# Four-layer graph network, layer 1: maximum over eight blocks, factors in two parts, negation on GpSimd, norms and skips at other items

## The chip, the cores and the metric

The kernel runs on one core of a Trainium2 chip. The metric is device time in microseconds of one execution; the time before is the median of three runs. The engines are named as in the profile: PE is TensorE's matmul and PEld its weight load, DVE is VectorE, ACT is ScalarE, POOL is GpSimd and SP is SyncE, which issues the DMAs.

## The reference

Four layers, each added to its input and followed by a layer norm over the 128 features. There are 3125 nodes and 103125 directed edges. Layer 0 is a weighted sum over neighbours. Layer 1, which the change touches, is an attention over edges with four heads of 32 features:

```python
h = (x @ W).reshape(n, HEADS, C)
a_s = jnp.einsum('nhc,hc->nh', h, att_src)
a_d = jnp.einsum('nhc,hc->nh', h, att_dst)
e = jax.nn.leaky_relu(a_s[src] + a_d[dst], NEG_SLOPE)
p = jnp.exp(e - m[dst])                      # m: the segment's maximum
out = segment_sum(h[src] * (p / z[dst])[:, :, None], dst)   # z: segment sum of p
out = out + gat_bias + x @ skip_W + skip_b
out = (out - mu) * rsqrt(var + EPS_LN) * ln_g + ln_b
x = layernorm(x + out)
```

Layer 2 is a dot-product attention and layer 3 two mean aggregations with a sigmoid.

## The kernel before, in words

The edges are turned into dense matrices: `wd` holds the weighted adjacency for layer 0 and `f_ctd` the edge counts (bf16) for layers 1 to 3. Nodes lie in 25 blocks of 128, `NB`. `general_path` is a fallback that doesn't run here; all the work is `fast_path`.

**Layer 0 to layer 1.** Layer 0's sums of blocks 0 to 19 (`Z0` = 20) end first; those of blocks 20 to 24 (`acc1`, tiles `left0` and `left1`) are still to be added from source blocks `ZA` = 6 to 24. The loop `for i in range(NB)` adds them (`add0`, line L862) and runs layer 1's preparation between, by a table `marks` of what is to be done at which `i`. `end0` adds the residual (L874) and normalises x. `scores1(g)` takes four blocks: transposes x (L1047), multiplies by the attention vectors (L1292, L1299), copies the destination scores out (L1301) and stores them to DRAM (L1302). `heads` copies the source scores to `sa` (L1307). `top` takes their maximum over all 20 blocks (L1401, then `highest` and `spread` by way of TensorE, L1081 to L1091), which gives `km`, the number that is subtracted ahead of the exponentials. The result doesn't depend on it as long as no exponential overflows; `in_range` looks after that. `factors` makes the exponentials of 20 blocks at once (L1315 to L1329).

`values(b)` makes the product operand `vp` of two blocks: x times W (L1336), scaled by the two factors (L1340), then split into three bf16 parts, each a cast on ScalarE and a subtraction on VectorE (L565 to L570 in `split3`), and last, a negated copy of the second half of the columns (L1350, one instruction a block). Eight pairs are made in the loop over `i`, at 9, 11, ..., 23, and five more inside head 0.

**The items.** Layer 1 then runs over `items` (g, h, c): two groups of destination blocks (`IG`, 12 and 13), four heads, 25 source blocks c: 200 items. `masks` makes for an item which edges take which branch of the leaky ReLU: an ACTIVATE on ScalarE (L1384) and a minimum on VectorE (L1388), or for some items one instruction on VectorE (L1380); one item in five of the later heads also has L1391. `products` multiplies count matrix and mask with `vp` (L1449, L1453), summing in PSUM over c. At the end of a head, `sums` reduces (L1482) and GpSimd finishes (L1490 to L1495); `quotients` divides nine items later (L1499 to L1505, items of 1.6 to 1.9 us).

`later(k, f)` puts `f` into a list that `step()` runs k items later; what step() starts stands behind the last mask and product already issued on its engine. `skips` (L1463, L1466) computes x times `skip_W` for four blocks at a time into `r`. `finished` runs the norms of group 0 under the items of group 1: `finish1` for four blocks is a first norm (L1116 to L1120, a root on ScalarE, then L1209 and L1210) and a second norm with its scaling on ScalarE (L1141) or, with `on_v`, on VectorE (L1134). `turns1` transposes the new x (L1150) and multiplies by layer 2's weights (L1158). `unit`, `doubled` (L1258) and `bound2` prepare layer 2. PSUM's banks are named acc0 to acc4, tr_sa, left0 and left1; `bank()`, which highest, skips and turns use, is acc1 alone in layer 1.

What order the instructions take on an engine is set by the framework's scheduler from readiness and from the order of the program; `tc.issue_after(i)` puts the instructions of a block behind `i` on that engine.

Of the kernel before, what the change touches and what calls it, by code (L numbers as in the profile page):

```python
# [13 lines left out]
OP = mybir.AluOpType  # L14
AX = mybir.AxisListType
# [4 lines left out]
NB = 25  # L20
# [499 lines left out]
def fast_path(  # L520
# [351 lines left out]
    def end0(acc, b0, n):  # L872
        i = x[:, b0 : b0 + n, :]
        nc.vector.scalar_tensor_tensor(i, acc[:, 0:n, :], 0.0, i, OP.max, OP.add)  # L874
        layer_norm(lp0, i, i, (0, n), True)

    zp = front.enter_context(tc.tile_pool(name="f_zp", bufs=4))
# [186 lines left out]
    def later(k, f):  # L1064
        due.append((now[0] + k, f))
# [21 lines left out]
    def spread(d, n, o):  # L1087

        t = bank()
        nc.tensor.matmul(t[:, 0:n], ones, d, start=True, stop=True)  # L1090
        nc.vector.tensor_copy(o, t[:, 0:n])  # L1091
# [168 lines left out]
    with ExitStack() as st:  # L1260
# [43 lines left out]
        def heads(t, b0, n):  # L1304

            b = slice(b0, b0 + n)
            nc.vector.tensor_copy(sa[:, b, :], t[:, 0 : n * 2 * H].rearrange("p (b h) -> p b h", h=2 * H))  # L1307
            nc.vector.tensor_scalar(nas[:, b], sa[:, b, 0:H], -1.0, None, OP.mult)
            nc.gpsimd.tensor_scalar(bas[:, b], sa[:, b, 0:H], UP, None, OP.mult)
# [21 lines left out]
        def values(b):  # L1331
# [17 lines left out]
            for k in range(n):  # L1349
                nc.vector.tensor_scalar(  # L1350
                    vp[:, b + k, :, :, 2 * F1 : 3 * F1], vp[:, b + k, :, :, F1 : 2 * F1], -1.0, None, OP.mult
                )
# [41 lines left out]
        spare.append(lambda: zps.tile([P, 512], F32, name="few", tag="acc1"))  # L1394
        marks = {ZA - 1: lambda: [scores1(g) for g in range(Z0 // 4)]}
        keep = {}

        def top():
            heads(t8, 0, Z0)
            ex = fp.tile([P, H], F32, name="ex", bufs=1)  # L1400
            nc.vector.tensor_reduce(ex, sa[:, 0:Z0, 0:H].rearrange("p b h -> p h b"), AX.X, OP.max)  # L1401
            keep["d"] = highest(fp, ex, H)

        marks[ZA] = top
        marks[ZA + 2] = lambda: (spread(keep["d"], H, km), factors(0, Z0))
        ready = 0
        for i in range(NB):
            if i >= ZA:
                add0(cp, i, acc1, (Z0, NB - Z0), "ct1")
            if i in marks:  # L1410
                marks[i]()
            if i in (19, 21, 23):
                masks(*items[(i - 19) // 2])
            if i > ZA + 2 and i % 2:
                values(ready)
                ready += 2
        sp = st.enter_context(tc.tile_pool(name="f_sp1", bufs=2))
# [4 lines left out]
        for g, (b0, n) in enumerate(left):  # L1422
            end0(acc1[g], b0, n)
        def in_range():
# [48 lines left out]
        def sums(acc, g, h):  # L1473
# [39 lines left out]
            def finished():  # L1513
                for k, b in enumerate(range(0, n, 4)):
                    later(15 * k, lambda b=b: finish1(sp, i0 + b, min(4, n - b), 2, False))
                    later(15 * k + 12, lambda b=b: turns1(sp, i0 + b, min(4, n - b), 5))
                later(2, lambda: unit(i0, n))
                later(58, lambda: doubled(i0, n))
                later(57, lambda: bound2(sp, 0))

            later(1 if last else 9 if g or h else 18, quotients)
            if (g, h) == (0, H - 1):
                later(20, finished)

# [3 lines left out]
        for x_, (g, h, c) in enumerate(items):  # L1528
# [4 lines left out]
            if (g, h, c) == (0, 1, 0):  # L1533
                lag[0] = 4
            if (g, h, c) in ((0, 1, 0), (1, 0, 1)):
                later(0, lambda: skips(i0, i0 + n))
            if (g, h, c) == (0, 2, 12):
# [19 lines left out]

            if c < NB - 1:
                more_masks()
# [492 lines left out]
```

## Time and profile before

| | |
|---|---|
| median of 3 runs | 1314.13 us (1310.74 to 1314.8) |
| profiled execution | 1310.76 us, of which the span of instructions is 1309.0 us |
| busy, share of the span | PE 94%, PEld 84%, DVE 73%, ACT 66%, POOL 22% |
| mean granted TensorE clock | 0.993 |
| layer 0's last sums, blocks 0 to 19 | end at 409.5 us |
| layer 1's products | 446.9 to 805.8 us |
| ends of heads (first and last L1482), group 0 | 499 to 505, 542 to 546, 580 to 584, 618 to 621 us |
| ends of heads, group 1 | 663 to 668, 712 to 718, 761 to 765, 801 to 806 us |
| set of norms of group 0 (first L1116 of each `finish1`) | 657.9, 688.4, 719.0 us |

The profile is of one execution. "Busy" of TensorE includes matmuls that are pipelined, so its idle time is the sure reading; the idle time stands in the timeline in brackets ahead of an instruction, with the name of what ended it. A stretch's row gives its length, then the busy time and count of each engine, the granted clock, the DMA engines' share and GB/s.

### The profile page before, as it was taken

The page shows a single profiled execution, that of the slowest core. Times are in us where ns is not written, and L with a number is a line of the kernel's source. Part 1 is how long each engine was busy: PE and PEld are TensorE (multiplying, and loading weights), DVE is VectorE, ACT ScalarE, POOL GpSimd, SP SyncE. Part 2 cuts the span into 40 slices and gives each one's busy share as a digit, 9 for nine tenths or more (in the row PEclk, how much of TensorE's full clock was granted, in tenths as well). Part 3 has the DMA queues.
Part 4 walks back from the last instruction along what each step waited for, and adds up shares of the span by engine and source line. Part 5 has one row for each costly group of instructions (what it writes and reads, how often), then busy time and mean ns, then how long its engine had stood idle before and what let it go on. Part 6 is the DMA issues. An engine that isn't in the chain of part 4 may idle for free.

```text
span 1309.0 us, 31168 instructions
## 1 busy us (share of the span) xinstructions
PE 1235.2 (94%) x13072; PEld 1102.6 (84%) x13072; DVE 953.5 (73%) x1420; ACT 866.1 (66%) x1364; POOL 284.5 (22%) x219
## 2 busy tenths in 40 slices
PE   4999999999999998999989999999999999999995
PEld 3899999999997888999989897777777777876785
DVE  6989999999934898899889987843474347332365
ACT  2977787777744797999788996544474444543455
POOL 6904526091002242222211322000000000000011
PEclk9999999999999999999999999999999999999998
DMA  7579898988997766888877775522222223861674
GB/s 184 148 223 285 239 273 264 277 258 252 289 307 235 252 206 212 282 282 281 252 250 237 236 244 175 199 68 73 62 75 76 75 64 101 258 205 49 203 220 134
DMA packets 192261, 261.95 MB, mean 200 GB/s; under 512 B 16844, under 2 KB 135802, under 8 KB 191982
## 3 DMA queue, kind: packets, MB, share of 16 engines
q1 hardware_dynamic: 191085, 257.42, 64.1%
q8 instruction: 104, 1.70, 0.5%
q0 software_dynamic: 720, 1.97, 0.5%
q10 hardware_dynamic: 305, 0.48, 0.1%
q14 instruction: 47, 0.39, 0.1%
HBM read 196.72 MB, written 63.10 MB: 198 GB/s over the span
## 4 chain that ended last, share of the span: by engine, by line
PE 70%; DVE 11%; ACT 8%; DMA 3%; issue 3%; POOL 1%; SPq 1%; POOLq 0%; DVEq 0%; ACTq 0%
PE acc L1453 11%; PE acc L1672 11%; PE s L1664 10%; PE wp L961 7%; PE acc L1449 6%; PE acc L862 6%; PE acc L1772 5%; PE cp L953 3%; PE acc L1854 3%; ACT wod L925 2%; DVE cm L1388 2%; ACT cm L1384 2%; ACT cs L966 1%; DVE wod L918 1%; DMA ct<-f_ctd 1%
## 5 line engine op out<-in xcount | busy, mean ns | idle before, releaser
L1449 PE MATMUL acc<-vp,ct 128*128 128x99 bf16 (+1 forms) x2500 | 323.2, 209 | 7.6 <-DVE vp L1350 5.1
L1453 PE MATMUL acc<-vp,cm 128*128 128x198 bf16 (+1 forms) x2500 | 324.6, 244 | 5.2 <-DVE cm L1388 5.1
L1384 ACT ACTIVATE cm<-adr,bas 128x1536 bf16<-128x1536 f32 (+1 forms) x184 | 286.4, 1619 | 31.4 <-PE acc L1453 22.3
L1453 PEld LDWEIGHTS <-cm 128*128 128x128 bf16 x2500 | 239.6, 97 | 16.4 <-issue 8.8
L1449 PEld LDWEIGHTS <-ct 128*128 128x128 bf16 x2500 | 242.2, 98 | 1.1 <-DVE ct L1391 0.6
L1388 DVE TENSOR_TENSOR cm<-cm,ct 128x1536 bf16<-128x1536 bf16 (+1 forms) x184 | 195.3, 1087 | 24.3 <-ACT cm L1384 20.0
L1668 DVE TENSOR_TENSOR e<-e,ct 128x512 f32<-128x512 f32 (+2 forms) x175 | 107.5, 623 | 105.3 <-ACT e L1667 100.5
L1667 ACT ACTIVATE e<-s,f_nm 128x512 f32<-128x512 f32 (+2 forms) x175 | 109.4, 633 | 109.4 <-PE s L1664 105.1
L961 PE MATMUL wp<-wod,ohc 128*128 128x128 f16 x2512 | 167.7, 220 | 14.8 <-ACT cs L966 12.2
L1672 PEld LDWEIGHTS acc<-self__6449,e 128*128 128x128 f32 x1250 | 147.4, 192 | 21.5 <-issue 13.1
L961 PEld LDWEIGHTS <-ohc 128*128 128x128 f16 x2512 | 149.1, 98 | 15.7 <-issue 15.2
L918 DVE TENSOR_TENSOR wod<-ohd,w 128x4096 f16<-128x4096 f16 (+1 forms) x82 | 161.6, 2009 | 0.0
L1672 PE MATMUL acc<-self__6449,e 128*128 128x129 f32 x1250 | 147.9, 275 | 1.8 <-DVE e L1668 1.8
L862 PE MATMUL acc<-f_xw,cw 128*128 128x128 f32 x1000 | 143.6, 284 | 4.1 <-DMA cw<-wd 4.1
L1664 PE MATMUL s<-yT,f_xT 128*128 128x512 f32 (+2 forms) x350 | 140.0, 539 | 0.1
L862 PEld LDWEIGHTS acc<-f_xw,cw 128*128 128x128 f32 x1000 | 123.6, 193 | 4.7 <-DMA cw<-wd 4.7
L966 ACT CAST cs<-cp 128x500 bf16<-128x500 f32 x157 | 90.4, 576 | 51.5 <-PE cp L953 50.6
L1615 ACT CAST cr<-ct 128x1590 fp32r<-128x1590 bf16 (+3 forms) x51 | 72.3, 1418 | 76.8 <-PE acc L1772 39.0
L925 ACT ACTIVATE wod<-ohd,wt 128x128 f16<-128x128 f16 x312 | 106.5, 398 | 9.5 <-DVE ohd L907 9.4
L1664 PEld LDWEIGHTS s<-yT,f_xT 128*128 128x128 f32 x350 | 62.8, 190 | 48.4 <-issue 21.5
L972 ACT COPY ws<-wp 128x512 f32<-128x512 f32 x157 | 88.0, 585 | 17.1 <-PE wp L961 17.0
L1617 DVE CAST cr<-ct 128x1536 fp32r<-128x1536 bf16 (+2 forms) x59 | 53.8, 915 | 62.5 <-PE acc L1772 31.5
(355 smaller groups left out, 1697.8 us busy)
## 6 DMA issues: line engine op xcount, KB each, us to landing
ct<-f_ctd SPq DMA_DIRECT2D x186, 384.0 KB
ct<-f_ctd SPq DMA_DIRECT2D x100, 416.0 KB
wd<-ws SPq DMA_DIRECT2D x39, 896.0 KB
cw<-wd SPq DMA_DIRECT2D x50, 640.0 KB
f_ctd<-cs SPq DMA_DIRECT2D x9, 2000.0 KB
ct<-f_ctd SPq DMA_DIRECT2D x25, 397.2 KB
ct<-f_ctd SPq DMA_DIRECT2D x22, 397.5 KB
ct<-f_ctd SPq DMA_DIRECT2D x25, 269.5 KB
```

What stands on the lines that cost most here:

```text
L862: steps.append(lambda j=j, a=cw[:, j - h, :]: nc.tensor.matmul(accs[j // 4][:, j % 4, :], a, xw[:, i, :], start=False, stop=(i == NB - 1 a ...
L918: tip[s] = nc.vector.tensor_tensor(packed(f, ww), packed(ohd, ww), twos(w2[s])[:, ww], OP.mult)
L925: nc.scalar.activation(wod[1][:, BW + w, :], ohd[:, BW + w, :], AF.Copy, scale=wl[:, 1, at : at + 1])
L961: tip["made"] = made = nc.tensor.matmul(wp[:, j, :], ohc[:, w, :], wod[s][:, w, :], start=(j == 0 and q == 0 and s == 0), stop=(j == 3 and ...
L1384: pins["a"] = nc.scalar.activation(m[:, : n * P], adrs[g, h][:, : n * P], AF.Relu, bias=bas[:, c, h : h + 1], scale=UP)
L1388: pins["v"] = nc.vector.tensor_tensor(m[:, : n * P], m[:, : n * P], ct[:, : n * P], OP.min)
L1449: nc.tensor.matmul(out_(F1, w), ct[:, k * P : (k + 1) * P], vp[:, c, h, :, 2 * F1 : F1 + w], start=(c == 0 and k % 2 == 0), stop=False, sk ...
L1453: pins["p"] = nc.tensor.matmul(out_(0, z), m[:, k * P : (k + 1) * P], vp[:, c, h, :, 0:z], start=False, stop=(c == NB - 1 and (k % 2 == 1 ...
L1664: nc.tensor.matmul(s[:, :m], xT[:, c * P : (c + 1) * P], yT[:, i0 * P + a : i0 * P + a + m], start=True, stop=True)
L1667: nc.scalar.activation(e[:, a : a + m], s[:, :m], AF.Exp, bias=nm[:, q : q + 1], scale=scale)
L1668: nc.vector.tensor_tensor(e[:, a : a + m], e[:, a : a + m], ct[:, a : a + m], OP.mult)
L1672: nc.tensor.matmul(acc[k // 3][:, (k % 3) * (P + 1) : (k % 3 + 1) * (P + 1)], es[q, c][:, k * P : (k + 1) * P], vo[:, c, 0 : P + 1], start ...
```

## The change

- `top` takes `heads` and the maximum over the first eight blocks, after two calls of `scores1`; the other three come at i = 8, 10 and 12, `heads` of blocks 8 to 19 at 13. `factors` runs for blocks 0 to 7 at i = 7 and for 8 to 19 at i = 14.
- Pairs of values are made at i = 8, 9, 11, 13, 15, 16, 18, 20 and 22: nine instead of eight.
- The negation L1350 goes from VectorE to GpSimd.
- `end0` gives back its addition, and the masks issued in the first three items stand behind the last of these on its engine.
- `finished` starts 10 items after the sums instead of 20. `finish1` starts at 0, 18 and 43 from there (before 0, 15, 30), with its second scaling on VectorE; `turns1` at 19, 43 and 50 (before 12, 27, 42); `bound2` and `doubled` at 68 and 70 (before 57 and 58).
- The skips of group 1's blocks run at the start of head 3 of group 0 instead of in item 1 of group 1.

```diff
     def end0(acc, b0, n):
         i = x[:, b0 : b0 + n, :]
-        nc.vector.scalar_tensor_tensor(i, acc[:, 0:n, :], 0.0, i, OP.max, OP.add)
+        added = nc.vector.scalar_tensor_tensor(i, acc[:, 0:n, :], 0.0, i, OP.max, OP.add)
         layer_norm(lp0, i, i, (0, n), True)
+        return added
...
             b = slice(b0, b0 + n)
-            nc.vector.tensor_copy(sa[:, b, :], t[:, 0 : n * 2 * H].rearrange("p (b h) -> p b h", h=2 * H))
+            z = b0 * 2 * H if b0 < Z0 else 0
+            nc.vector.tensor_copy(sa[:, b, :], t[:, z : z + n * 2 * H].rearrange("p (b h) -> p b h", h=2 * H))
...
             for k in range(n):
-                nc.vector.tensor_scalar(
+                nc.gpsimd.tensor_scalar(
                     vp[:, b + k, :, :, 2 * F1 : 3 * F1], vp[:, b + k, :, :, F1 : 2 * F1], -1.0, None, OP.mult
                 )
...
-        marks = {ZA - 1: lambda: [scores1(g) for g in range(Z0 // 4)]}
         keep = {}
 
         def top():
-            heads(t8, 0, Z0)
+            heads(t8, 0, 8)
             ex = fp.tile([P, H], F32, name="ex", bufs=1)
-            nc.vector.tensor_reduce(ex, sa[:, 0:Z0, 0:H].rearrange("p b h -> p h b"), AX.X, OP.max)
+            nc.vector.tensor_reduce(ex, sa[:, 0:8, 0:H].rearrange("p b h -> p h b"), AX.X, OP.max)
             keep["d"] = highest(fp, ex, H)
 
-        marks[ZA] = top
-        marks[ZA + 2] = lambda: (spread(keep["d"], H, km), factors(0, Z0))
+        def more_values():
+            nonlocal ready
+            values(ready)
+            ready += 2
+
         ready = 0
+        marks = {ZA - 1: lambda: [scores1(g) for g in range(2)], ZA: top}
+        marks[ZA + 1] = lambda: (spread(keep["d"], H, km), factors(0, 8))
+        marks[ZA + 2] = lambda: (more_values(), scores1(2))
+        marks[ZA + 3] = more_values
+        marks[ZA + 4] = lambda: scores1(3)
+        marks[ZA + 5] = more_values
+        marks[ZA + 6] = lambda: scores1(4)
+        marks[ZA + 7] = lambda: (more_values(), heads(t8, 8, Z0 - 8))
+        marks[ZA + 8] = lambda: factors(8, Z0 - 8)
+        for i in (15, 16, 18, 20, 22):
+            marks[i] = more_values
...
-            if i > ZA + 2 and i % 2:
-                values(ready)
-                ready += 2
...
         for g, (b0, n) in enumerate(left):
-            end0(acc1[g], b0, n)
+            added = end0(acc1[g], b0, n)
...
             def finished():
-                for k, b in enumerate(range(0, n, 4)):
-                    later(15 * k, lambda b=b: finish1(sp, i0 + b, min(4, n - b), 2, False))
-                    later(15 * k + 12, lambda b=b: turns1(sp, i0 + b, min(4, n - b), 5))
+                for b, k, t in zip(range(0, n, 4), (0, 18, 43), (19, 43, 50)):
+                    later(k, lambda b=b: finish1(sp, i0 + b, min(4, n - b), 2 if k < 43 else 1, True))
+                    later(t, lambda b=b: turns1(sp, i0 + b, min(4, n - b), 5))
                 later(2, lambda: unit(i0, n))
-                later(58, lambda: doubled(i0, n))
-                later(57, lambda: bound2(sp, 0))
+                later(70, lambda: doubled(i0, n))
+                later(68, lambda: bound2(sp, 0))
...
-                later(20, finished)
+                later(10, finished)
...
-            if (g, h, c) in ((0, 1, 0), (1, 0, 1)):
-                later(0, lambda: skips(i0, i0 + n))
+            if (g, h, c) in ((0, 1, 0), (0, 3, 0)):
+                later(0, lambda of=IG[h // 2]: skips(of[0], sum(of)))
...
-            if c < NB - 1:
+            if x_ < 3:
+                with tc.issue_after(added.ins):
+                    more_masks()
+            elif c < NB - 1:
                 more_masks()
```

## The prediction

> **What bounds the kernel now.** I read the page first, then busy time by stretch, cut at the reductions L1482 that end each head, then TensorE's timeline for the idle places, then groups by line for the prices.
>
> The page's first part says which engine to follow:
>
> ```profile
> PE 1235.2 (94%) x13072; PEld 1102.6 (84%) x13072; DVE 953.5 (73%) x1420; ACT 866.1 (66%) x1364; POOL 284.5 (22%) x219
> ```
>
> TensorE is busy 94% of the span, so the change can win only where TensorE waits. Layer 1's products run from 447 to 806 us. By stretch (length, then PE, PEld, DVE, ACT and POOL busy; PEclk is the granted clock):
>
> ```profile
> 447.00:503.00 56.00, 48.14 (x616) 45.05 (x614) 50.60 (x104) 46.70 (x58) 15.12 (x22) 0.94 0.64 200
> ...
> 584.00:621.00 37.00, 37.00 (x599) 37.00 (x596) 34.21 (x37) 35.26 (x25) 12.43 (x6) 1.00 0.88 288
> 621.00:668.00 47.00, 47.00 (x692) 46.95 (x690) 40.47 (x49) 35.22 (x23) 9.76 (x7) 1.00 0.81 254
> 668.00:718.00 50.00, 44.71 (x678) 43.35 (x676) 46.14 (x92) 43.26 (x44) 9.00 (x9) 1.00 0.74 235
> 718.00:765.00 47.00, 44.15 (x661) 43.04 (x659) 43.35 (x74) 41.11 (x44) 12.41 (x8) 1.00 0.72 226
> ```
>
> The first row is head 0 of group 0: TensorE idles 56.00 - 48.14 = 7.9 us and the clock is below 1, while VectorE is busy 50.6 of 56. The last four are head 3 of group 0 and heads 0, 1, 2 of group 1. TensorE loses nothing until 668, then 5.3 and 2.9 us, where VectorE is busy 46 of 50 and 43 of 47. These two places, 16 us of idle time, are what the change touches. TensorE's timeline says what it waited for:
>
> ```profile
> 451.49 0.25 PE L1449 MATMUL acc<-vp,ct 128*128 128x102 bf16 x1 [2.20 <-DVE f_x L874]
> 456.47 0.26 PE L1453 MATMUL acc<-vp,cm 128*128 128x198 bf16 x1 [0.48 <-DVE cm L1388]
> 487.70 0.21 PE L1449 MATMUL acc<-vp,ct 128*128 128x102 bf16 x1 [1.46 <-DVE vp L1350]
> 492.20 0.21 PE L1449 MATMUL acc<-vp,ct 128*128 128x102 bf16 x1 [1.16 <-DVE vp L1350]
> 498.09 0.21 PE L1449 MATMUL acc<-vp,ct 128*128 128x102 bf16 x1 [2.53 <-DVE vp L1350]
> 675.10 0.26 PE L1453 MATMUL acc<-vp,cm 128*128 128x198 bf16 x1 [3.09 <-DVE cm L1388]
> 730.28 0.26 PE L1453 MATMUL acc<-vp,cm 128*128 128x198 bf16 x1 [1.57 <-DVE cm L1388]
> ```
>
> In head 0 the last releaser is always VectorE: layer 0's last addition L874, which stood in its queue behind values; a mask; and three times the negation L1350 that ends a pair of values. The two in group 1 are masks late behind norms (L1209, L1210 stand just before at 669 and 727 us). Two idle places also cost clock:
>
> ```profile
> 451.40:454.70 3.30, 3.21 (x26) 3.01 (x26) 3.30 (x15) 1.86 (x4) 0.00 (x0) 0.50 0.18 73
> ...
> 499.10:502.50 3.40, 3.40 (x30) 3.16 (x29) 1.73 (x4) 0.07 (x1) 0.00 (x0) 0.50 0.31 116
> ```
>
> For 3.3 and 3.4 us after the waits of 2.20 and 2.53 the granted clock was 0.50, so some 1.7 us each is lost again. After the longer wait of 3.09 us at 672 the clock stayed at 1.00. The Trainium skill (TensorE: Matmul & The Clock Gate, Part 1) says that the clock is judged in free-running windows of about 3.4 us; by that rule it is chance which gap is punished. Recoverable in all: 7.9 + 3.4 + 8.1 = 19.4 us.
>
> **The change, part by part.**
>
> *Maximum over eight blocks, factors in two parts.* Before, the copy L1307 of the scores comes at 422.99, after all five groups, and the first value product L1340 at 427.26, 4.3 us later. Group 1's scores leave TensorE at 415.2 (L1299, 414.17 + 1.02), so now the first value can come at 415.2 + 4.3 = 419.5. What can delay it: the transpose in `highest` uses bank acc1, which group 1's L1299 fills and ScalarE's L1301 empties, before only at 418.88 to 419.44; from there (L1081 to L1340, 3.3 us) it is 422.8. So values start 4.5 to 7.7 us earlier; I take 6. VectorE has room: it idled 1.81 us before 415.64 and 5.70 us before 422.99. TensorE gains nothing before 447: L862 fills it there, and its work is only reordered. The added work is one more heads (about 0.3 + 0.2 us) and one more set of factors, under 2 us on VectorE and 1.1 us on ScalarE, in time that was idle. A wait of TensorE for acc1 could cost up to 3 us; L862 steps stand ready beside it, and I charge 0.8.
>
> In head 0, VectorE is relieved of what spilled past 447 (one L1340, two L567, three L569, at 0.41, 0.75 and 0.75 us: 4.2 us) and of one whole pair, since nine pairs instead of eight now stand ahead of the products (two L1340, one L567, one L569: 2.3 us). 50.6 - 6.5 = 44.1 us. TensorE's own work there is 56 - 7.9 - 3.4 - 0.4 (the pair's four L1336) = 44.3 us. The two come out level, so the waits shrink but don't all go. I take the 2.20 us behind L874 as gone with its clock loss of 1.65, and the 0.48. Of the last three waits (5.15 us) I keep 3: the last four pairs are issued at the same steps as before, four items (4 x 1.6 us) ahead of use, and their chain (L1340 0.8, then L565, L567, L568, L569, L570 at 0.63 to 0.75, then the negation) takes about as long. Half of the second clock loss goes, 0.85. Sum: 2.20 + 1.65 + 0.48 + 2.15 + 0.85 - 0.8 = **6.5 us**, between a loss of 3 (the acc1 wait, nothing else) and a gain of 11.3.
>
> *Negated values on GpSimd.* VectorE sheds 25 L1350, 5.8 us busy. GpSimd's price isn't in the trace. From below: its L1309 on 128x80 takes 0.42 us; from above, L733 and L736, one-input steps on 128x256, average 2.3 and 2.5 us while VectorE is saturated. The nearest rows are L1344 (128x256, 0.70) and L1490 (128x396, 1.55, two inputs); I take 0.9, so 22.5 us in all. It isn't free for VectorE: at 505.20 five L1388 took 6.49 us, 1.30 each, with GpSimd working beside them, against 0.95 alone. That is 0.27 us per us of GpSimd, or 6.1 us for 22.5: it eats the 5.8 saved. At 0.42 us each VectorE would gain 3; at 2.4 each it would lose 10. I put it at **0**. What it moves: a pair now ends with two GpSimd steps, 1.8 us instead of 0.45, part of the 3 us that I kept above.
>
> The Trainium skill (GPSIMD Engine Reference, 4.1 Engine selection, and 1. Specifications) speaks against this edit: element-wise work belongs on VectorE, and GpSimd shares its SBUF interfaces. It calls one-input work roughly line-rate. As an estimate from its 3.1, 396 elements at 1.8 cycles and 1.2 GHz take 0.6 us, by which the edit would win VectorE about 1.7 us.
>
> *`added`, masks of the first three items behind it.* Masks L1388 from 455.5 already stand behind L874 (454.63): 0, and nobody waits longer.
>
> *Norms between the changes of heads.* A set of four blocks costs VectorE, by groups from 621 to 765: L1116 1.7, L1118 0.7, L1120 0.8, L1209 1.9, L1210 1.4, reciprocals 0.3: 6.9 us. With the second scaling on VectorE instead of ScalarE (four times 0.34, as L1134 takes at 837 us) it is 8.2; ScalarE sheds 4 x 0.41 = 1.65 us a set (L1141 at 682). Sets now start 10, 28 and 53 items after the group's change instead of 20, 35 and 50, so one falls in each of heads 0, 1 and 2; in the kernel before head 1 holds nearly two. VectorE afterwards: head 0: 40.5 - 2.3 (skips) - 1.9 (L1116 and others already there) + 8.2 = 44.5 against TensorE's 47.0 - 1.5 = 45.5. Head 1: 46.1 - 6.0 (four of twelve L1116 and L1118, four of eight L1209 and L1210) + 1.4 = 41.5 against 44.7. Head 2: 43.4 + 1.4 = 44.8 against 44.2. So TensorE leads in two and VectorE by half a us in the third. Of 8.1 us idle I keep 3: **5 us** gained, between 0 and 8. The first set stands one item behind the quotients' GpSimd steps (L1501, L1505, some 3 us), so VectorE may wait a us for them; that is in the 3.
>
> *All skips in group one.* Thirteen L1463 (1.5 us of TensorE) and four L1466 (2.3 us of VectorE) move from 631 us to head 3 of group 0. TensorE's work is only moved. VectorE there goes from 34.2 to 36.5 of 38.5 us: cover enough. The wait for a skip's bank can recur (1.0 us at 513): I charge 0.5, between 0 and 1.2.
>
> **Sum.** 6.5 + 0 + 5 - 0.5 = 11 us. The profiled execution took 1310.76 us (span 1309.0), so 1299.8 on its own scale. That is 3.4 below the median of the three runs, 1314.13, and at their low end. On the median's scale 1314.1 - 11 = **1303** us is my number.
>
> **Rivals.**
> *GpSimd sets the pace (slower).* GpSimd works in order. If a pair's negations stand ahead of the next pair's copies L1343, the pairs no longer overlap: 0.8 + 1.9 of casts + 1.5 of subtractions + 0.4 to 0.8 of copies + two negations + waits between engines, about 6.4 us a pair at 0.9 each. Thirteen pairs from 420 end at 503, 5 us behind today's 498.3, just what the norms gain. That is the point from which it decides: above 0.9 us each, in order, it is a loss. At 1.2 us: 7.0 x 13 = 91, last value at 511, 13 late; 13 - 5 = 8 slower, 1322. Against it: today copies of the next pair (427.86) already run ahead of L1344 of the last (428.82), so the order interleaves.
> *Nothing gained (same).* The stalls only move: head 0 stays tied to the last four pairs' chain, VectorE is as late with masks in head 2, and 3 us or less are won: 1312.
> *One half works.* Only head 0 or only the norms: 5 to 6 us, 1308 or 1309. For it: the two stages share nothing but VectorE.
>
> **How the numbers follow.** Both halves 0.50; one half 0.20; nothing 0.14; slower 0.16. Faster by over 0.3% (4 us, about what a measurement of this kernel can tell from no change) is the first two, 0.70; within it 0.14; slower 0.16. The low end, 1295, takes nearly the whole 19.4 us. The high end, 1316, takes in the case of nothing gained and the mild end of the slow one.
>
> **What would show it.** Right: no half clock near 451; products from about 447 as now, head 0's L1482 near 496 instead of 499 to 505; first L1340 near 421; idle time of TensorE from 668 to 765 halved, group 1's last L1482 some 11 us earlier. Wrong: L1449 released by GpSimd in long waits, negations over 1.2 us each, L1388 means above 1.1 us in head 0, new waits of TensorE for bank acc1 at 415 to 420, or a mask late behind L1134-like scalings in head 2.

## The result and the profile after

The changed kernel takes 1319.72 us in the median of 18 runs (1314.22 to 1321.74); the kernel before took 1314.42 us beside it (18 runs, 1310.74 to 1318.94). The ratio is 1.0038, with a 95% interval of 1.0029 to 1.0047: about 5 us slower, where 11 us faster was forecast, and outside the range given (1295 to 1316).

The profiled execution took 1319.73 us, of which the span is 1317.8, at a mean granted clock of 0.988. That is 9.0 us over the profiled execution of before, which was one of that kernel's quickest. Part of the gap doesn't belong to the change: layer 0's sums end at 412.0 instead of 409.5 us, with one half-clock window (403.3 to 406.7) just before. So the two traces are compared below from layer 0's end on, stage by stage. The page's first part, after:

```profile
PE 1237.7 (94%) x13072; PEld 1104.1 (84%) x13072; DVE 959.2 (73%) x1413; ACT 862.3 (65%) x1356; POOL 320.3 (24%) x246
```

TensorE is as busy as before; GpSimd has 36 us more, 25 of its 27 new instructions being the negations. Line numbers moved a little: the negation is L1352 (L1350 before), the copies of factors L1345 (L1343), the self product L1346 (L1344), masks L1386, L1390 and L1393 (L1384, L1388, L1391), products L1462 and L1466 (L1449, L1453), sums L1495 (L1482), skips L1476 and L1479 (L1463, L1466), turns L1151 and L1159 (L1150, L1158), the copy of a turn's result L1168 (L1167), the scaling on VectorE L1135 (L1134), masks in one instruction L1382 (L1380).

Busy time by stretch, after: length, then PE, PEld, DVE, ACT and POOL busy, granted clock, DMA share, GB/s. The rows are head 0 of group 0 with what runs into it, head 3 of group 0, and heads 0, 1 and 2 of group 1:

```profile
449.40:510.70 61.30, 49.61 (x654) 46.57 (x653) 50.96 (x89) 51.30 (x62) 37.30 (x42) 0.94 0.61 190
592.60:632.10 39.50, 38.08 (x593) 37.88 (x591) 34.51 (x40) 33.63 (x23) 6.01 (x5) 1.00 0.79 251
632.10:675.20 43.10, 43.10 (x651) 43.10 (x649) 41.48 (x68) 33.76 (x24) 9.77 (x7) 1.00 0.84 274
675.20:722.00 46.80, 43.69 (x670) 42.61 (x668) 44.18 (x75) 39.75 (x35) 12.55 (x9) 1.00 0.76 249
722.00:774.40 52.40, 48.76 (x678) 46.49 (x676) 44.89 (x77) 41.28 (x44) 14.47 (x9) 0.93 0.65 205
```

Head 0 still leaves TensorE idle for 61.30 - 49.61 = 11.7 us, more than the 7.9 before, and GpSimd, which was busy 15 of 56 us there, is busy 37 of 61. Group 1's head 2 has 52.40 us, with 3.6 idle and the clock at 0.93. In TensorE's timeline after, the instructions that stood longest, with the idle time and its releaser in brackets:

```profile
457.43 0.25 PE L1462 MATMUL acc<-vp,ct 128*128 128x102 bf16 x1 [5.15 <-DVE f_x L874]
462.40 0.21 PE L1462 MATMUL acc<-vp,ct 128*128 128x102 bf16 x1 [1.76 <-DVE f_x L874]
500.38 0.21 PE L1462 MATMUL acc<-vp,ct 128*128 128x102 bf16 x1 [3.33 <-POOL vp L1352]
599.30 1.13 PE L1476 MATMUL few<-f_l_swt,f_xT 128*128 128x128 f32 x8 [1.42 <-DVE f_xw L1479]
742.35 0.22 PE L1462 MATMUL acc<-vp,ct 128*128 128x99 bf16 x1 [1.33 <-DVE ct L1393]
745.73 1.08 PE L1151 MATMUL few<-f_ident,f_x 128*128 128x128 f32 x4 [1.88 <-DVE self__6449 L1168]
```

The wait behind L874, which the forecast took as gone, is there and larger (2.20 before, 5.15 and 1.76 now). The waits for the last pairs, whose releaser is now GpSimd's negation, add up to 4.5 us (5.15 before, of which the forecast kept 3), the longest 3.33 (2.53). Two are new and have to do with bank acc1: a skip in head 3 of group 0 and a turn in head 2 of group 1. Around the first wait the clock is at half (same columns as the stretches above):

```profile
403.30:406.70 3.40, 3.40 (x19) 3.40 (x18) 2.02 (x10) 0.00 (x0) 0.00 (x0) 0.50 1.13 221
454.50:461.30 6.80, 3.22 (x24) 2.82 (x24) 4.35 (x10) 3.45 (x7) 6.33 (x10) 0.50 0.21 86
```

The first row is the window in layer 0 named above; the second lies across the end of the 5.15 us wait.

In us from layer 0's end, the lengths of the stages by the ends of the last reduction of each head, for before, after, and three kernels of the experiments below:

| | before | after | a_neg_dve | c_turns | d_skips6 |
|---|---|---|---|---|---|
| to the end of head 0, group 0 | 95.8 | 98.6 | 91.3 | 91.3 | 91.3 |
| heads 1 and 2 | 79.1 | 79.4 | 79.5 | 78.9 | 79.4 |
| head 3 (skips of group 1 are now here) | 37.4 | 42.0 | 42.0 | 41.9 | 40.4 |
| group 1, head 0 | 46.5 | 43.1 | 43.1 | 43.1 | 43.1 |
| head 1 | 49.9 | 46.6 | 46.6 | 47.8 | 47.9 |
| head 2 | 46.9 | 52.6 | 51.7 | 48.1 | 48.1 |
| head 3 | 41.2 | 41.2 | 41.2 | 41.2 | 41.2 |
| sum | 396.8 | 403.5 | 395.4 | 392.3 | 391.4 |

None of the three parts wins in sum: head 0 loses 2.8 where 6.5 were to be won; head 1 of group 1 wins 3.3 but head 2 loses 5.7, of which 0.9 isn't there in a_neg_dve, whose head 2 has no half clock; and head 0 of group 1 wins 3.4 that head 3 of group 0 loses with 1.2 more.

### The profile page after: what moved, and what is told of

It is laid out like the page before. It is cut to its first block, busy times and chain, and to the rows that moved or that the text cites. A ratio compares the mean times of both kernels' runs of the same rounds, so it can differ in the third digit from the quotient of the medians.

```text
span 1317.8 us, 31189 instructions
## 1 busy us (share of the span) xinstructions
PE 1237.7 (94%) x13072; PEld 1104.1 (84%) x13072; DVE 959.2 (73%) x1413; ACT 862.3 (65%) x1356; POOL 320.3 (24%) x246
## 4 chain that ended last, share of the span: by engine, by line
PE 67%; DVE 12%; ACT 7%; DMA 4%; issue 4%; POOL 3%; DVEq 0%; ACTq 0%; SPq 0%; POOLq 0%
PE acc L1688 11%; PE s L1680 10%; PE acc L1466 9%; PE wp L962 7%; PE acc L862 6%; PE acc L1462 5%; PE acc L1788 5%; PE acc L1870 4%; PE cp L954 3%; DVE cm L1390 3%; DVE wod L919 2%; ACT cm L1386 2%; ACT wod L926 2%; DMA wd<-ws 2%; DMA ct<-f_ctd 2%
## 5 line engine op out<-in xcount | busy, mean ns | idle before, releaser
L1462 PE MATMUL acc<-vp,ct 128*128 128x99 bf16 (+1 forms) x2500 | 323.5, 209 | 12.7 <-DVE f_x L874 6.9
L1466 PE MATMUL acc<-vp,cm 128*128 128x198 bf16 (+1 forms) x2500 | 325.1, 244 | 1.0 <-DVE cm L1390 0.9
L1386 ACT ACTIVATE cm<-adr,bas 128x1536 bf16<-128x1536 f32 (+1 forms) x184 | 287.0, 1619 | 43.1 <-PE acc L1466 34.2
L1466 PEld LDWEIGHTS <-cm 128*128 128x128 bf16 x2500 | 240.3, 97 | 16.4 <-issue 9.7
L1462 PEld LDWEIGHTS <-ct 128*128 128x128 bf16 x2500 | 242.8, 98 | 2.4 <-DVE ct L1393 1.9
L1390 DVE TENSOR_TENSOR cm<-cm,ct 128x1536 bf16<-128x1536 bf16 (+1 forms) x184 | 201.3, 1121 | 26.4 <-ACT cm L1386 24.4
```

Source lines behind the costliest of these rows:

```text
L1386: pins["a"] = nc.scalar.activation(m[:, : n * P], adrs[g, h][:, : n * P], AF.Relu, bias=bas[:, c, h : h + 1], scale=UP)
L1390: pins["v"] = nc.vector.tensor_tensor(m[:, : n * P], m[:, : n * P], ct[:, : n * P], OP.min)
L1462: nc.tensor.matmul(out_(F1, w), ct[:, k * P : (k + 1) * P], vp[:, c, h, :, 2 * F1 : F1 + w], start=(c == 0 and k % 2 == 0), stop=False, sk ...
L1466: pins["p"] = nc.tensor.matmul(out_(0, z), m[:, k * P : (k + 1) * P], vp[:, c, h, :, 0:z], start=False, stop=(c == NB - 1 and (k % 2 == 1 ...
```

## The experiments

The theory after the result: the negation on GpSimd is the loss, and the rest of the front is a gain. Rivals: that the front itself is too early for the engines around it; that the norms' and skips' new places are the loss; and, inside the first theory, which of three things makes it, the small copies that stand behind negations in GpSimd's queue, the last pairs' longer chain, or VectorE slowed by its neighbour. Every ratio is to the kernel before on the same chip in the same rounds; runs of one group share a chip, so a comparison across groups crosses chips and rests on the ratios alone. Where two experiments are compared with each other, the difference of their ratios is given with the root of the summed squares of the half intervals.

### First group: one part at a time

**Negation back on VectorE (a_neg_dve).**

```diff
-                nc.gpsimd.tensor_scalar(
+                nc.vector.tensor_scalar(
                     vp[:, b + k, :, :, 2 * F1 : 3 * F1], vp[:, b + k, :, :, F1 : 2 * F1], -1.0, None, OP.mult
```

> The changed kernel with the negation L1352 back on VectorE and all else as changed. Theory G (GpSimd's in-order queue paces the values: each negation takes 1.45 us there, the next pairs' copies L1345 stand behind it): copies no longer wait, ScalarE's casts L565 wait under 1 us in all, the addition L874 of left0 comes within 1 us of the last L862 sum, no 5 us wait of TensorE near 452, head 0 ends 5 to 8 us earlier, ratio to the kernel before 0.995 to 1.000. Rival F (the new order of factors and scores delays the values, whoever negates): head 0 ends where it does in the changed kernel within 1.5 us, ratio 1.003 to 1.005.

Measured: 0.9968 (0.9954 to 0.9982), median 1311.56 us, profiled span 1306.7. One word turns 0.4% slower into 0.3% faster: 0.0070 ± 0.0017 of 1314 us, 9 us. The trace shows 7.3 of them in head 0 (98.6 to 91.3 us) and the half-clock windows of after gone. TensorE's waits in head 0 of this kernel, by what was waited for (sum in us, times, longest):

```profile
PE acc L1462 <- DVE vp L1352: 3.7, 3, 1.6
PE acc L1462 <- DVE f_x L874: 1.9, 2, 1.0
PE acc L1466 <- DVE cm L1382: 0.5, 1, 0.5
```

And the same view of after:

```profile
PE acc L1462 <- DVE f_x L874: 6.9, 2, 5.1
PE acc L1462 <- POOL vp L1352: 4.5, 4, 3.3
PE tr L1048 <- ACT f_x L840: 0.3, 1, 0.3
```

5.0 us are lost behind L874, which is VectorE's addition and not the negation itself, and 0.8 behind the last pairs. With the half-clock window (6.80 us, of which TensorE was busy 3.22, so some 1.6 us of work lost), less the mask's 0.5 and with the 0.3 of the last row, that makes 7.2 us: the difference in head 0.

**The kernel before with the negation on GpSimd, and nothing else (b_neg_pool).**

```diff
-                nc.vector.tensor_scalar(
+                nc.gpsimd.tensor_scalar(
                     vp[:, b + k, :, :, 2 * F1 : 3 * F1], vp[:, b + k, :, :, F1 : 2 * F1], -1.0, None, OP.mult
```

> The kernel before with the negation alone moved to GpSimd. Theory G: the wait behind L874 near 450 grows from 2.2 to 4 us or more, GpSimd's copies L1343 wait behind negations of about 1.4 us, head 0 ends 4 to 8 us later than before, ratio 1.003 to 1.006. Rival F: the negation is harmless without the new order, ratio 0.998 to 1.002.

Measured: 1.0005 (0.9991 to 1.0019), median 1317.72 us, span 1310.2. The theory missed here: the same edit that costs 9 us in the changed kernel costs 0.7 ± 1.8 us by time in the old one, though the trace has 3.2 us more in head 0 (99.0 against 95.8). TensorE's waits there:

```profile
PE acc L1449 <- POOL vp L1350: 6.6, 4, 3.7
PE acc L1449 <- DVE f_x L874: 2.5, 1, 2.5
PE acc L1453 <- DVE cm L1388: 1.8, 1, 1.8
```

The waits for the last pairs have grown (5.1 before, in three), but the one behind L874 has hardly (2.2). The traces show a difference between the two kernels, in GpSimd's queue. GpSimd's timeline of this kernel (start, length, what; x2 is two in a row):

```profile
432.42 0.32 POOL L1343 COPY v<-fa 128x8 f32<-128x8 f32 x2
432.70 0.61 POOL L1344 TENSOR_TENSOR self__6449<-v,own 128x256 f32<-128x256 f32 x1
433.28 2.85 POOL L1350 TENSOR_SCALAR vp<-vp 128x396 bf16<-128x396 bf16 x2
436.08 1.05 POOL L1343 COPY v<-fa 128x8 f32<-128x8 f32 x2
```

The same view of after:

```profile
440.50 2.77 POOL L1352 TENSOR_SCALAR vp<-vp 128x396 bf16<-128x396 bf16 x2
...
445.49 3.20 POOL L1352 TENSOR_SCALAR vp<-vp 128x396 bf16<-128x396 bf16 x2
448.64 0.96 POOL L1345 COPY v<-fa 128x8 f32<-128x8 f32 x4
452.11 5.74 POOL L1352 TENSOR_SCALAR vp<-vp 128x396 bf16<-128x396 bf16 x4 [1.36 <-ACT vp L570]
457.79 0.57 POOL L1345 COPY v<-fa 128x8 f32<-128x8 f32 x4
```

In the old order every pair's copies, 0.16 and 0.53 us each in these rows, run between two pairs of negations. In the new one four copies (two pairs' worth) stand behind 3.2 and then 5.7 us of negations. The next pair's first cast on ScalarE needs them. ScalarE's timeline of after, with the idle time:

```profile
443.44 1.17 ACT L565 CAST vp<-v 128x528 bf16<-128x528 f32 x2 [2.88 <-POOL v L1345]
449.39 0.63 ACT L565 CAST vp<-v 128x528 bf16<-128x528 f32 x1 [2.25 <-POOL v L1345]
458.14 0.63 ACT L565 CAST vp<-v 128x528 bf16<-128x528 f32 x1 [2.53 <-POOL v L1345]
```

That is 7.7 us in which ScalarE waited for an 0.2 us copy; the view of waits of b_neg_pool has no such row, nor has that of before. The subtractions behind these casts are VectorE's, and L874 stands behind them: it starts, from layer 0's end, at 44.7 us in after, at 40.5 in a_neg_dve and 42.1 in b_neg_pool.

**Old norms in the new kernel (a_norms_back)**, with their old items, the scaling on ScalarE and the old places of `doubled` and `bound2`:

```diff
-                for b, k, t in zip(range(0, n, 4), (0, 18, 43), (19, 43, 50)):
-                    later(k, lambda b=b: finish1(sp, i0 + b, min(4, n - b), 2 if k < 43 else 1, True))
-                    later(t, lambda b=b: turns1(sp, i0 + b, min(4, n - b), 5))
+                for k, b in enumerate(range(0, n, 4)):
+                    later(15 * k, lambda b=b: finish1(sp, i0 + b, min(4, n - b), 2, False))
+                    later(15 * k + 12, lambda b=b: turns1(sp, i0 + b, min(4, n - b), 5))
...
-                later(10, finished)
+                later(20, finished)
```

> The changed kernel with the norms of group 0 at their old items, scaled on ScalarE, and turns, bound and doubling at their old items. Theory N (the new places cost: the third set's transposes start 7 items after the second's and want the one bank acc1 that these still hold, 2 us and a half clock at 744): heads 0 to 2 of group 1 take together no longer than in the changed kernel, the wait before L1151 at 743 goes, ratio 0.999 to 1.003. Rival B (the new places gain the 3 to 5 us that were forecast and the loss in head 2 is luck of the clock): ratio 1.006 to 1.008.

Measured: 1.0032 (1.0015 to 1.0050), median 1320.58 us, span 1314.1. Against the changed kernel 0.0006 ± 0.0020 less: the norms' new places neither lost nor won anything that this can show, where 5 us were forecast as won. Heads 0, 1 and 2 of group 1 have 43.5, 50.1 and 46.9 us (old norms) against 43.1, 46.6 and 52.6 (new): what head 1 wins, head 2 loses. Both traces have half clock in these heads, 3.4 us in head 1 here and 6.8 in head 2 there.

**Old skips in the new kernel (a_skips_back).**

```diff
-            if (g, h, c) in ((0, 1, 0), (0, 3, 0)):
-                later(0, lambda of=IG[h // 2]: skips(of[0], sum(of)))
+            if (g, h, c) in ((0, 1, 0), (1, 0, 1)):
+                later(0, lambda: skips(i0, i0 + n))
```

> The changed kernel with group 1's skips back in item 1 of group 1. Theory S (the move to head 3 of group 0 costs a wait for bank acc1, 1.4 us at 598, and ScalarE or VectorE are too full there; only 1.5 us of TensorE work should have moved): head 3 of group 0 is 2.5 to 4 us shorter, head 0 of group 1 1.5 to 2 longer, ratio 1.001 to 1.003. Rival (moved work only): sum of the two heads unchanged within 1 us, ratio 1.003 to 1.005.

Measured: 1.0025 (1.0010 to 1.0040), median 1319.78 us, span 1318.5. 0.0013 ± 0.0017 less than the changed kernel: unclear. In its profiled execution head 0 took 102.1 us with 17.1 us of half clock (13.7 in one stretch, 3.4 in another), before the skips' places matter, so its span says nothing on them; head 3 of group 0 and head 0 of group 1 took 37.6 and 46.1 against 42.0 and 43.1, 1.4 us less in sum.

So the negation is the loss; no other part shows one by its time, to within some 2.5 us each.

### Second group: inside the two losses

**Copies of the factors on ScalarE (a_copies_act)**, so that none stands behind a negation:

```diff
-                nc.gpsimd.tensor_copy(v[:, :, :, s * F1 + C], fa[:, s, b : b + n])
+                nc.scalar.copy(v[:, :, :, s * F1 + C], fa[:, s, b : b + n])
```

> The changed kernel with the two small copies of each pair (L1345, column C of v) on ScalarE instead of GpSimd; the negation stays on GpSimd. Theory Q (queue order: the 7 us are the next pairs' copies held behind negations of 1.4 us in GpSimd's queue, and with them ScalarE's casts L565): casts no longer wait for GpSimd, the addition L874 of left0 follows the last L862 sum within 3 us (7 us in the changed kernel), head 0 ends 4 to 7 us earlier than in the changed kernel, ratio 0.997 to 1.000. Rival C (contention: GpSimd's 36 us of negation slow VectorE's own instructions beside them, wherever the copies stand): head 0 ends within 2 us of the changed kernel's, ratio 1.002 to 1.005.

Measured: 1.0019 (1.0001 to 1.0036), median 1319.49 us, span 1314.3. By the trace head 0 falls from 98.6 to 95.2 us, L874 starts at 40.8 instead of 44.7, and TensorE's wait behind it falls from 6.9 to 1.3 us; ScalarE's casts wait for GpSimd no more. TensorE's waits in head 0:

```profile
PE acc L1462 <- POOL vp L1352: 4.5, 4, 1.9
PE acc L1466 <- DVE cm L1390: 1.6, 1, 1.6
PE acc L1462 <- DVE f_x L874: 1.3, 1, 1.3
```

By time it is 0.0019 ± 0.0020 less than the changed kernel: of the trace's 3.4 us, between 0 and 5 are in the ratio. The theory of the queue expected 4 to 7 us and a ratio of at most 1.000, its rival under 2 us and 1.002 to 1.005: the trace shows that the queue has a part in the loss, and the time doesn't settle how large it is. Head 1 of group 0 has 2.3 us more, with a half-clock window of 3.4 us at 511.8, which takes most of it back in this execution.

**Negation on VectorE for early pairs, on GpSimd for the last ones (a_late_pool)**, block 18 being the first of the four pairs that are made inside head 0:

```diff
-                nc.gpsimd.tensor_scalar(
+                (nc.gpsimd if b >= 18 else nc.vector).tensor_scalar(
```

> The changed kernel with the negation on GpSimd only for blocks 18 to 24 (the four late pairs inside head 0), on VectorE for the nine early pairs. Theory Q: the harm is done by the early pairs, whose negations stand between copies; head 0 as in the kernel with all negations on VectorE, within 2 us, ratio 0.995 to 0.999. Rival (the last step of the late pairs, two or more times 1.4 us, is what TensorE waits for): head 0 ends 3 us or more later than with all on VectorE, ratio 0.999 to 1.002.

Measured: 0.9990 (0.9975 to 1.0004), median 1314.36 us, span 1312.3. 0.0048 ± 0.0017 less than the changed kernel, 0.0022 ± 0.0020 more than a_neg_dve. So the 18 early negations cost 6 ± 2 us and the last seven 3 ± 3, which lies between the two expectations. The trace agrees: head 0 has 98.6, 94.1 and 91.3 us in after, this one and a_neg_dve, 4.5 and 2.8 apart. Of the 2.8, 1.0 is longer waits for the last pairs (4.7 against 3.7) and 1.7 a half-clock window of 3.4 us that began 0.6 us after the longest of them, of 3.33 us; the same 3.33 us in after had none behind it. Its waits in head 0 are for the last pairs those of after, behind L874 those of a_neg_dve:

```profile
PE acc L1462 <- POOL vp L1352: 4.7, 3, 3.3
PE acc L1462 <- DVE f_x L874: 1.9, 2, 1.0
```

**New norms in the old kernel (b_norms)**, the reverse of a_norms_back:

```diff
-                    later(15 * k, lambda b=b: finish1(sp, i0 + b, min(4, n - b), 2, False))
-                    later(15 * k + 12, lambda b=b: turns1(sp, i0 + b, min(4, n - b), 5))
+                    later(k, lambda b=b: finish1(sp, i0 + b, min(4, n - b), 2 if k < 43 else 1, True))
+                    later(t, lambda b=b: turns1(sp, i0 + b, min(4, n - b), 5))
...
-                later(20, finished)
+                later(10, finished)
```

> The kernel before with the new items of norms and turns alone and their scaling on VectorE. Theory N: heads 0 to 2 of group 1 take as long in sum as before or up to 3 us longer (head 1 about 3 less, head 2 about 5 more), ratio 1.000 to 1.003. Rival B (the forecast 3 to 5 us are there, only hidden by the moved skips): ratio 0.996 to 0.998.

Measured: 0.9998 (0.9981 to 1.0014), median 1313.99 us, span 1311.4. Nothing, again. Heads 0, 1 and 2 of group 1: 46.1, 46.6 and 51.7 us, 144.4 in sum against 143.3 before.

**Second set's turns nine items earlier (c_turns)**, on top of a_neg_dve, so that they fall in head 1 (item 10 + 34 = 44) instead of head 2 (item 53):

```diff
-                for b, k, t in zip(range(0, n, 4), (0, 18, 43), (19, 43, 50)):
+                for b, k, t in zip(range(0, n, 4), (0, 18, 43), (19, 34, 50)):
```

> The changed kernel with the negation on VectorE (0.9968) and the second set's turns 34 items after the start of the norms instead of 43, so that it has given bank acc1 back before the third set's turns at 50. Theory N (head 2 of group 1 loses its 5 us to the two overlapping sets of turns and the one bank): the waits of 2.0 and 1.8 us before L1151 and L1159 at 733 to 739 go, head 2 falls from 51.7 to 46 to 48 us, head 1 rises by 1 to 2, ratio 0.993 to 0.996. Rival V (VectorE is too full in head 2 with the scaling and the late norms, bank or not): head 2 stays above 50 us, ratio 0.996 to 0.998.

Measured: 0.9946 (0.9925 to 0.9966), median 1308.20 us, span 1304.8. Against a_neg_dve 0.0022 ± 0.0025 less: the time leans that way and doesn't settle it. The trace does say where it would come from. Heads 1 and 2 of group 1 in a_neg_dve (columns as above):

```profile
664.90:711.60 46.70, 43.59 (x668) 42.51 (x667) 44.08 (x76) 39.65 (x35) 12.53 (x8) 1.00 0.77 249
711.60:763.30 51.70, 46.38 (x681) 44.27 (x678) 45.06 (x77) 41.46 (x44) 14.54 (x9) 1.00 0.68 209
```

and in c_turns:

```profile
665.30:713.10 47.80, 44.70 (x673) 43.41 (x670) 44.65 (x75) 39.98 (x36) 13.38 (x9) 1.00 0.74 244
713.10:761.30 48.20, 45.07 (x675) 43.52 (x674) 44.72 (x78) 41.00 (x43) 14.47 (x8) 1.00 0.70 223
```

Some 1.2 us of TensorE's work moves from head 2 to head 1, and head 2's idle time falls from 5.3 to 3.1 us while head 1's stays at 3.1: 98.4 us become 96.0. In head 2 the wait of a turn for the other set's copy out of bank acc1 (1.88 us, L1151 behind L1168) is gone, with 1.3 us behind a mask L1393, and one of 1.68 behind L549 is 0.45; there are instead 1.51 us of L1159 behind L1168 and 1.2 behind the scaling L1135. What the bank alone was worth isn't separated.

### Third group: what is left, and the best version

**The front alone in the old kernel (b_front)**: maximum over eight blocks, factors in two parts, nine pairs ahead, the order behind `added`; negation on VectorE, old norms, old skips. Its edit is the change without these:

```diff
-                nc.vector.tensor_scalar(
+                nc.gpsimd.tensor_scalar(
...
-                later(20, finished)
+                later(10, finished)
...
-            if (g, h, c) in ((0, 1, 0), (1, 0, 1)):
-                later(0, lambda: skips(i0, i0 + n))
+            if (g, h, c) in ((0, 1, 0), (0, 3, 0)):
+                later(0, lambda of=IG[h // 2]: skips(of[0], sum(of)))
```

> The kernel before with the front alone: maximum over eight blocks, factors in two parts, nine pairs ahead of the products, the first masks behind the last addition; negation on VectorE, norms and skips as before. If the front's part of the forecast was right in mechanism (values 6 us earlier, VectorE no longer the limit of head 0), head 0 ends 4 to 5 us earlier relative to layer 0's end and everything after it is as before: ratio 0.995 to 0.998. If the gain of the changed kernel with VectorE's negation came from norms or skips instead: ratio 0.999 to 1.001.

Measured: 0.9947 (0.9928 to 0.9966), median 1309.96 us, span 1309.2. Timed, the front with VectorE's negation is worth 7.0 ± 2.5 us. By the trace 4.5 of them are in head 0 (95.8 to 91.3). The rest isn't seen in this execution, which had half clock in layer 0 (400.9) and for 6.8 us in head 2 of group 1 (728.6); its span alone would have said "same".

**Skips back on top of c_turns (d_skips_back)**, the edit of a_skips_back again:

```diff
-            if (g, h, c) in ((0, 1, 0), (0, 3, 0)):
+            if (g, h, c) in ((0, 1, 0), (1, 0, 1)):
```

> The kernel with negation on VectorE and the second set's turns at 34 (0.9946), and group 1's skips back in group 1. Theory S (the move costs more than it gives, 4.5 us in head 3 of group 0 against 3 us in head 0 of group 1): ratio 0.992 to 0.995, head 3 back at 37.5 us and head 0 of group 1 at 46. Rival (the skips' place gives room to the first set of norms): head 0 of group 1 above 47.5 us, ratio 0.995 to 0.998.

Measured: 0.9950 (0.9933 to 0.9967), median 1309.70 us, span 1303.7; the same as c_turns. Head 3 of group 0 and head 0 of group 1 take 38.2 and 46.1 us, 84.3 in sum; in c_turns 41.9 and 43.1, 85.0. Moving the skips moved their time. Their price on TensorE stands in the trace of before, in its old place (622 to 655 us):

```profile
L1463 PE MATMUL few<-f_l_swt,f_xT 128*128 128x128 f32 x26 | 3.6, 278 | 0.0
```

**Skips six items later (d_skips6)**, on top of c_turns:

```diff
-            if (g, h, c) in ((0, 1, 0), (0, 3, 0)):
+            if (g, h, c) in ((0, 1, 0), (0, 3, 6)):
```

> The same kernel (0.9946) with group 1's skips begun six items later in head 3 of group 0. Theory S2 (the skips' loss there is the wait of 1.5 us for bank acc1, whose emptying L1479 stands behind a burst of masks that GpSimd's end-of-head work slows): the wait before the second L1476 falls below 0.4 us, head 3 takes 40 to 40.7 us instead of 41.9, ratio 0.992 to 0.995. Rival (any four skips in this head meet a full VectorE): head 3 stays above 41.3 us, ratio 0.994 to 0.997.

Measured: 0.9931 (0.9914 to 0.9949), median 1307.46 us, span 1304.9. This is the best version: 0.0069 or 9 us faster than the kernel before, and 0.0107 ± 0.0020 or 14 us faster than the changed one. Against c_turns it is 0.0015 ± 0.0027 less, unclear by time alone. In the trace the wait is gone that the skips at the head's first item had. The skips' group in c_turns (busy, mean ns, then the idle time before them):

```profile
L1476 PE MATMUL few<-f_l_swt,f_xT 128*128 128x128 f32 x26 | 3.7, 281 | 1.3 <-DVE f_xw L1479 1.3
```

and in d_skips6:

```profile
L1476 PE MATMUL few<-f_l_swt,f_xT 128*128 128x128 f32 x26 | 3.6, 278 | 0.0
```

In c_turns the first four blocks' skips leave TensorE at 580.6, but the copy L1479 that empties bank acc1 starts only at 588.55: VectorE has just done five of the reductions that end a head (577.72 to 580.29) and then runs five masks L1390 and one L1393 that were due. The next skips, issued one item after the copy, find the bank full and wait to 589.38. With the start six items later VectorE has caught up; the copy is at 595.62 and the next skips, at 597.11, wait for nothing. Head 3 falls from 41.9 to 40.4 us, that wait and a little.

**Second scaling back on ScalarE (d_scale_act)**, on top of c_turns:

```diff
-                    later(k, lambda b=b: finish1(sp, i0 + b, min(4, n - b), 2 if k < 43 else 1, True))
+                    later(k, lambda b=b: finish1(sp, i0 + b, min(4, n - b), 2 if k < 43 else 1, False))
```

> The same kernel (0.9946) with the second scaling of group 0's norms on ScalarE as before (L1141 instead of L1135). If ScalarE was the short one, as the forecast had it: heads 0 to 2 of group 1 together 2 to 5 us longer, ratio 0.996 to 0.999. If VectorE was: 1 to 3 us shorter, ratio 0.992 to 0.994. If neither: within 1 us.

Measured: 0.9956 (0.9940 to 0.9971), median 1310.17 us, span 1304.5. 0.0010 ± 0.0026 more than c_turns; heads 0 to 2 of group 1 take 140.0 us against 139.0. Which engine scales hardly matters.

## Why the prediction was wrong

**The front was right in its direction and near its size, but not by the terms of the sum.** The first product of values starts 11.6 us after layer 0's end instead of 17.7: 6.1 earlier, 6 were taken. Without the negation's move, head 0 is 4.5 us shorter by the trace and the kernel 7.0 ± 2.5 us faster by time (b_front), where 6.5 were summed. The waits, though, fell only from 7.8 us (2.20 + 0.48 + 5.15) to 6.1 in a_neg_dve, where 4.8 were to go: the 2.20 behind L874 and the 0.48 that were taken as gone are still there as 1.9 (in two) and 0.5, and for the last pairs 3.7 are left where 3 were kept. The larger part is the half clock: the two windows of before cost some 3.3 us, where 2.5 were summed, and head 0 has none in the traces of all six kernels with this front and VectorE's negation; none of the waits listed for a_neg_dve is over 1.6 us, where before had 2.20 and 2.53. The 0.8 charged for a wait for bank acc1 at 415 us wasn't needed: between 405 and 447 us TensorE waits only 0.2 us in all, for another bank.

**The step that failed: "I put it at 0", the negation on GpSimd.** The price taken was 0.9 us; the trace has 25 at a mean of 1445 ns (minimum 1212):

```profile
L1352 POOL TENSOR_SCALAR vp<-vp 128x396 bf16<-128x396 bf16 x25 | 35.6, 1445 | 6.0 <-ACT vp L570 6.0
```

Of the two rows weighed for it, the nearer one was L1490 (128x396, 1.55, two inputs), not L1344 (128x256, 0.70): one input and bf16 made it hardly cheaper here. The count of elements alone doesn't give it either (0.70 x 396/256 is 1.08), and why it takes 1.45 stays open. The Trainium skill (GPSIMD Engine Reference, 4.1 Engine selection) calls one-input work roughly line-rate, and the estimate from the best case in its 3.1 was 0.6 us; the measurement is twice that at its least. Its general advice, to keep element-wise work on VectorE, is what a_neg_dve's 9 us bear out, in this order of the work; in the old order the same move cost 0.7 ± 1.8.

But the size alone is not the mechanism. The prediction's sum set VectorE's relief (5.8 us) against VectorE's slowing (6.1), and so looked at the wrong engine. VectorE did not become the trouble: the groups of subtractions L567 and L569 take 21.6 us in after's head 0,

```profile
L567 DVE TENSOR_TENSOR vs<-v,vp 128x528 f32<-128x528 f32 (+1 forms) x13 | 11.7, 921 | 4.2 <-ACT vp L570 2.0 <-ACT vp L565 1.9
L569 DVE TENSOR_TENSOR vs<-vs,vp 128x528 f32<-128x528 f32 (+1 forms) x13 | 9.9, 773 | 0.4 <-ACT vp L568 0.4
```

against 9.5 and 9.3 in a_neg_dve, 2.8 us more, less than the 7.1 that its 25 L1352 cost there. So VectorE was relieved, and head 0 grew all the same. What was lost stood in two queues. Early, copies of 0.2 us behind negations of 2.8 to 5.7, with casts, subtractions and L874 behind them: 4.5 us of head 0 by a_late_pool (6 timed), 3.4 by a_copies_act. Late, a pair that ends with two GpSimd steps instead of two VectorE steps: 2.8 us (3 timed), 1.7 of it by half clock. This is the rival "GpSimd sets the pace", which was priced 8 us slower at 1.2 us each and given 0.16, with its point of decision, 0.9 us, at just the price that was taken. Its size didn't come true: by its own sum 1.45 us each make a pair 7.5 us and the last value 19 us late, but the last negation ended 95.1 us after layer 0's end against 88.9 before, 6.2 later. So the pairs did not stop overlapping altogether, as the rival had it; three casts waited. The reason then set against it, that the old order interleaves copies with other GpSimd work, holds for the old order: b_neg_pool, where the queue does interleave, lost 0.7 ± 1.8 us. The front that the prediction welcomed changed that order, and the step that used the old order as evidence didn't ask whether it still held. That the order is the whole difference between 0.7 and 9 us was not shown by a run of its own; the 7.7 us of casts waiting, present in the one and absent in the other, speak for it.

**The norms: 5 us forecast, nothing found** (b_norms 0.9998, a_norms_back 1.0032 against 1.0038). VectorE's sum for head 2 was right: 44.9 us in after, 44.8 worked out (44.2 against 41.5 in head 1). The step that failed is "one falls in each of heads 0, 1 and 2". It counted the norms and not the turns that follow them: the second set's at item 10 + 43 = 53 and the third's at 60 are both in head 2, one behind the other's copy out of the single bank acc1. TensorE's work there, put at 44.2, was 46.4 (a_neg_dve), and it idled 5.3 besides. Head 1 won the 3.3 us and head 2 lost 4.8. Of the 5 us, c_turns gets 2.4 back by the trace.

**The skips: 0.5 charged.** Head 3 grew by 4.6 us and head 0 of group 1 shrank by 3.4, so 1.2 net by the traces, at the upper bound given. Most of both is the moved work, which the forecast undercounted: thirteen L1463 and 1.5 us of TensorE, where the trace of before has 26 and 3.6. The wait named as possible did recur, at 1.42 us instead of 1.0. By time the two places can't be told apart (0.9950 and 0.9946).

**The sum** was thus 6.5 + 0 + 5 - 0.5 = 11 forecast, and 4.5 - 7.3 - 1.5 - 1.2 = -5.5 by the stages of the traces (the norms' -1.5 being heads 1 and 2 of a_neg_dve against before), with 5 us slower timed. The stages of after alone make 6.7; the other 1.2 are the 0.9 of head 2 named above and 0.3 in heads 1 and 2 of group 0.

## What to carry to other kernels

Work moved to an idle engine has two prices, its own length and the length of what stands behind it there: list everything small in that engine's queue, and who waits for it, in the order that the changed program will give, not in that of the old trace. When a set of steps is moved, follow it to its last step and resource (here the turns and their one bank), because the part that was moved to fit may push the part behind it onto a neighbour. And one execution can be several us off by half-clock windows: head 0, which is the same in after, a_norms_back and a_skips_back, took 98.6, 99.0 and 102.1 us with 6.8, 10.2 and 17.1 us of half clock. So a change of a few us is told from stage lengths and repeated times together.

## What the runs showed of the hardware

The length of a gap alone did not decide the clock: a gap of 3.33 us left it at 1.00 in after (ended 500.38) and a gap of the same 3.33 us in a_late_pool (ended 492.78) was followed by 3.4 us at 0.51. The rows after the two gaps, after first:

```profile
500.40:507.20 6.80, 6.09 (x88) 5.82 (x88) 5.11 (x7) 4.42 (x6) 5.24 (x5) 1.00 0.68 234
493.40:496.80 3.40, 3.40 (x30) 3.20 (x29) 2.35 (x3) 1.51 (x2) 3.40 (x4) 0.51 0.56 195
```

A gap of 3.66 us in b_neg_pool (ended 494.36) went with 6.8 us of half clock from 493.0, and the one of 5.15 us in after ended inside such a window. The Trainium skill (TensorE: Matmul & The Clock Gate, Part 1) describes windows of about 3.4 us that run freely; all half-clock stretches seen here were 3.4 us or a multiple of it, up to 13.7, which fits. That it was the phase of the window that told the two gaps apart isn't shown by a run.

GpSimd took 1.21 to 2.42 us in after, 1.45 in the mean, for a multiply by a constant on 128x396 bf16, where VectorE took 0.28 (before) to 0.33 (a_neg_dve) in the mean for the same instruction: four to five times as long. VectorE's 26 subtractions were slowed by 2.8 us in all with 36 us of such work on GpSimd, 0.08 us for each us. That is not the 0.27 that the masks of the kernel before had suggested, because VectorE's subtractions ran beside only part of that work: the 18 full-size subtractions of after that ran wholly beside GpSimd work took 0.92 us in the mean (0.70 to 1.23), the three with none beside them 0.70, so 0.24 us for each us side by side.
